# Key statistics counted a cycle earlier, the norms' bound in cycle 4, two banks for the last outputs, the verdict ahead of the last additions, and a looped general path

## The chip, the cores and the metric

The kernel runs on one core of one Trainium2 chip. The metric is the device time in microseconds (us) of that core: 1371.79 us is the median of three runs (1371.77, 1371.79 and 1372.5).

## What is computed

The input is `x` of 32 batches, each of 256 tokens with 256 channels, and a context of 32 batches of 77 tokens. Two gated blocks follow each other, all in float32:

```python
x = x + tanh(g_xattn) * attention(layernorm(x), ctx, ctx)   # 8 heads of 128
x = x + tanh(g_ffn)   * ffn(layernorm(x))                   # 16 heads of 16

# attention, for every head: no softmax over the keys
mixed = cw * cos(q, k) + vw * cos(q, k) * decorr + ww * ratio(q) * ratio(k)
ratio(f) = 2 * min(var(f), 1) / (var(f) + 1)      # of a head's 128 features
# cw, vw, ww, decorr: four numbers a head, from statistics over all batches

# ffn, for every head: a softmax over the queries
z = softmax(k q') v, heads side by side, times Wo
z = z / max(|z|, 1e-12)
z = z @ Wff
z = z / max(|z|, 1e-12)
x = x + tanh(g) * gelu(z)
```

Two things of it matter here. Of every key token and head the kernel needs the norm and the ratio, thus mean and variance of 128 features. And of the two normalizations at the end the first cancels in the second as long as neither norm meets its lower limit of 1e-12: the kernel multiplies Wo by Wff once and normalizes once. Whether that was allowed is judged at the end, from a bound on the norms. If it was not, a general path computes the end of the block again from what the kernel has kept in DRAM.

## The kernel before

**Order.** Five engines work side by side: PE multiplies into PSUM, ACT does the exponentials and some copies, DVE the rest of the elementwise work, POOL powers and scalings, SP issues the transfers. PE, ACT, DVE and POOL take their instructions in the order in which the program lists them (`InOrder`). SP's order is the framework's. So an instruction that waits holds up all that stand behind it on its engine.

**Stages.** A prologue computes the statistics over all batches. Then come software-pipelined cycles, one for each batch `n`. The list `cycle` names the stages of a cycle, each with the batch it works on relative to `n`: `(0, scores, 1)` is the feed-forward attention of batch `n`, `(1, ...)` the cross-attention of the next one, `(2, ...)` and `(3, ...)` the preparation of later ones, `(-1, ...)` the end of the last one. The two last batches have lists of their own, `last_but_one` and `last`. The function `run` calls a stage only once for each batch.

**The stages that the change touches or that stand around it.**

- `key_features(3)` computes features of keys by 128 rows, in the middle of a cycle, into `fvx` (four buffers). 77 rows to a batch and 128 to a tile: 20 tiles in all, the first two in the prologue, so 18 of the cycles have one to measure. `measure_keys(2)`, in the next cycle, runs `head_stats`: eight `bn_stats` (tile `kst`, one a head), then small operations on 128x8 values (tiles `kt`, `nrx`) on DVE and a power on POOL. `align_keys(2)` moves features and statistics to the batch's own rows by transfers of SP.
- Around `measure_keys` DVE has: the copy of `u` (`ff_out(-1)`), then the keys' operations, then `sums` and `vz` (`scale_values`), then the copy of `fq` out of PSUM (`query_features(2, 0, 1)`), whose bank PE writes again in `query_scores` (matmuls `mm<-fqT,fvT`).
- At the end of a cycle DVE has: two transposes `fb<-fq` (`turn_queries(2, 1)`), then `sums` and `vz` of `scale_values(0, 3)`, which waits for the last exponentials `e` of ACT. PE reads `vz` in `mix_values(-1, 3)` (matmuls `zp<-e,vz`), which opens the next cycle.
- `fetch_queries` brings the transposed query features back (`fqT<-fd`) for the `query_scores` of the next cycle.
- `ff_out` multiplies by the product of Wo and Wff (`mm<-w_of,zT`), both halves `t` of the tokens into one PSUM bank; ACT squares each half and sums it into `ny`, DVE copies the bank to `u`.
- `bound_norms` stands in `last`: ACT squares and sums two weights (tile `fb`), PE sums over the partitions (`mm<-bn,ones`), DVE makes the bound `low` of it. `judge`, after the last stage, compares all norms with it and leaves `verdict`, which every engine loads and branches on.
- `pass_time(n, k)` lets PE do `k` products that nobody reads (`mm<-winT,ident`). `last` has two of these.
- `mend`, the general path, is written out for all 32 batches behind the branch.
- `mm_tile` gives one of three PSUM banks in turn: a product waits until the third one before it was read.

Of the kernel before, what the change touches and what calls it, by code (L numbers as in the profile page):

```python
# [8 lines left out]
F32 = mybir.dt.float32  # L9
AF = mybir.ActivationFunctionType  # L10
# [4 lines left out]
P = 128  # L15
H = 8
# [19 lines left out]
def gated_block_kernel(  # L36
# [24 lines left out]
    nc = tc.nc  # L61
    B, S, D = x.shape
    M = cx.shape[1]
    NT = S // P
    NTOK = B * S
    NCTX = B * M
# [4 lines left out]
    pa = ctx.enter_context(tc.tile_pool(name="pa", bufs=2))  # L71
# [7 lines left out]
    pe, act, dve, pool = (  # L79
        InOrder(tc, e) for e in (nc.tensor, nc.scalar, nc.vector, nc.gpsimd)  # L80
    )
# [4 lines left out]
    o_v = out.rearrange("b (p t) d -> p b t d", t=NT)  # L86
# [31 lines left out]
    ny = const.tile([P, B, NT], F32, name="ny")  # L118
# [7 lines left out]
    def rsqrt_of(r, v):  # L126

        rows, n = v.shape
        pool.tensor_tensor(r, v, nhalf[0:rows, 0:n], ALU.pow)
# [11 lines left out]
    def mm_tile():  # L141
        return ps.tile([P, 512], F32, tag="mm", name="mm")

    def head_stats(src, rows, n, tag):

        st = pa.tile([rows, n, 6], F32, tag=f"{tag}st", name=f"{tag}st")
        for i in range(n):
            dve.bn_stats(st[:, i, :], src(i))
        t = pa.tile([rows, 4, n], F32, tag=f"{tag}t", name=f"{tag}t")
        s, d, m2, n2 = (t[:, i, :] for i in range(4))  # L150
        dve.tensor_tensor(s, st[:, :, 1], st[:, :, 4], ALU.add)
        dve.tensor_tensor(d, st[:, :, 1], st[:, :, 4], ALU.subtract)
        dve.tensor_tensor(m2, st[:, :, 2], st[:, :, 5], ALU.add)
        dve.scalar_tensor_tensor(d, d, P / 4.0, d, ALU.mult, ALU.mult)
        dve.scalar_tensor_tensor(s, s, P / 4.0, s, ALU.mult, ALU.mult)
        dve.tensor_tensor(m2, m2, d, ALU.add)
        dve.tensor_tensor(n2, m2, s, ALU.add)

        dve.tensor_scalar(d, m2, P - 1.0, None, ALU.add)
        dve.reciprocal(d, d)  # L160
        return m2, n2, d
# [26 lines left out]
    z_kept = dram.tile([P, B, 2, S], F32, tag="z_kept", name="z_kept", bufs=1)  # L188
    x_kept = dram.tile([P, B, NT, D], F32, tag="x_kept", name="x_kept", bufs=1)
# [4 lines left out]
    fvx = []  # L194
# [7 lines left out]
    def run(b, stage, *which):  # L202
        key = (b, stage.__name__, which)
        if key not in given:
            given.add(key)
            stage(b, *which)
# [62 lines left out]
    def halves_due(b):  # L269
        def least(b):  # L270
            return 2 * ((min(b, B - 1) * M + M - 1) // P + 1)

        return max(least(b), (least(b) + least(b + 1) + 1) // 2) if b >= 0 else 0
# [16 lines left out]
                )  # L290
            act.copy(fv[:, hh * 512 : (hh + 1) * 512], pf[0:rows, :])

    def measure_keys(b):

        for i in range(halves_due(b - 1) // 2, halves_due(b) // 2):
            rows = min(P, NCTX - i * P)
            fv = fvx[i % 4][0:rows]
            nr = nrx[0:rows, i % 4, :]
            m2, n2, rt = head_stats(lambda h: fv[:, h * P : (h + 1) * P], rows, H, "k")
            pool.tensor_tensor(nr[:, 0:H], n2, nquart[0:rows], ALU.pow)  # L300
            dve.scalar_tensor_tensor(nr[:, H : 2 * H], m2, P - 1.0, rt, ALU.min, ALU.mult)

# [136 lines left out]
    def scale_queries(b, t):  # L439

        k = kept[b]
        fq = k["fq", t]
        m2, n2, rt = head_stats(lambda h: fq[:, h * P : (h + 1) * P], P, H, "q")
        rq = pa.tile([P, H], F32, tag="rq", name="rq")
        rsqrt_of(rq, n2)
        fq_h = fq.rearrange("p (h d) -> p h d", d=P)
        pool.tensor_tensor(
            fq_h, fq_h, rq.unsqueeze(2).to_broadcast([P, H, P]), ALU.mult
        )
        dve.scalar_tensor_tensor(  # L450
            qrps[b % 2][t][:, :, MR], m2, P - 1.0, rt, ALU.min, ALU.mult
        )
# [209 lines left out]
    def ff_out(b):  # L662

        k = kept[b]
        pu = mm_tile()
        for t in range(NT):
            for c in range(2):
                pe.matmul(
                    pu[:, t * D : (t + 1) * D], lhsT=k["zT"][:, c, t * P : (t + 1) * P],
                    rhs=w_of[:, c, D : 2 * D], start=(c == 0), stop=(c == 1),  # L670
                )
        u = [P, NT, D], F32
        k["u"] = sw.tile(*u, tag="wf_n", name="u") if b == B - 1 else pa.tile(*u, tag="u", name="u")
        for t in range(NT):
            ge = pa.tile([P, D], F32, tag="ge", name="ge")
            act.activation(
                ge, pu[:, t * D : (t + 1) * D], AF.Square, accum_out=ny[:, b, t : t + 1]
            )
        dve.tensor_copy(k["u"].rearrange("p t c -> p (t c)"), pu)

    def ff_keep(b):

# [7 lines left out]
    def bound_norms(b):  # L690


        bn = pa.tile([P, 2], F32, tag="bn", name="bn")
        for i, w in enumerate((ffw["v"], w_of[:, :, 0:D])):
            ge = pa.tile([P, 2, D], F32, tag="fb", name="fb", bufs=2)
            act.activation(ge, w, AF.Square, accum_out=bn[:, i : i + 1])
        pt = mm_tile()
        pe.matmul(pt[:, 0:2], lhsT=ones, rhs=bn, start=True, stop=True)
        dve.tensor_copy(bn, pt[:, 0:2])
        dve.tensor_scalar(  # L700
            low, bn[:, 0:1], bn[:, 1:2], 4.0 * TINY * (S * D**0.5) ** 2, ALU.mult, ALU.mult
        )
        dve.tensor_scalar(low, low, LEAST, None, ALU.max)

    def judge():

        ok = pa.tile([P, B * NT], F32, tag="ge", name="ok")
        n_f = ny.rearrange("p b t -> p (b t)")
        dve.tensor_scalar(ok, n_f, low[:, 0:1], None, ALU.is_ge)
        dve.scalar_tensor_tensor(ok, n_f, MOST, ok, ALU.is_le, ALU.mult)  # L710
        dve.tensor_reduce(bad, ok, AX.X, ALU.min)
        pt = mm_tile()
        pe.matmul(pt[0:1, 0:1], lhsT=bad, rhs=ones[:, 0:1], start=True, stop=True)
        dve.tensor_scalar(verdict, pt[0:1, 0:1], -1.0, float(P), ALU.mult, ALU.add)

    def mend(b):
        zT = pa.tile([P, 2, S], F32, tag="zT", name="zT", bufs=1)
        nc.sync.dma_start(out=zT, in_=z_kept[:, b])
        xt = pa.tile([P, NT, D], F32, tag="x", name="x", bufs=8)
        nc.sync.dma_start(out=xt, in_=x_kept[:, b])  # L720
        for t in range(NT):
            pu = mm_tile()
            for c in range(2):
                pe.matmul(
                    pu, lhsT=zT[:, c, t * P : (t + 1) * P], rhs=w_of[:, c, :],
                    start=(c == 0), stop=(c == 1),
                )
            nn = pa.tile([P, 2], F32, tag="bn", name="nn")
            u = pa.tile([P, 2, D], F32, tag="u", name="u")
            act.activation(u[:, 0], pu[:, 0:D], AF.Square, accum_out=nn[:, 0:1])  # L730
            i1 = rsqrt(pa, nn[:, 0:1], 1, "rs2", least=TINY)
            dve.tensor_scalar(u[:, 0], pu[:, D : 2 * D], i1[:, 0:1], None, ALU.mult)
            act.activation(u[:, 1], u[:, 0], AF.Square, accum_out=nn[:, 1:2])
            i2 = rsqrt(pa, nn[:, 1:2], 1, "i2", least=TINY)
            act.activation(u[:, 0], u[:, 0], AF.Gelu, scale=i2)
            dve.scalar_tensor_tensor(xt[:, t], u[:, 0], tg[:, 1:2], xt[:, t], ALU.mult, ALU.add)
        nc.sync.dma_start(out=o_v[:, b], in_=xt)

    def ff_gelu(b):
        k = kept[b]  # L740
# [351 lines left out]
    for g in range(NG):  # L1092
# [4 lines left out]
        for i in range(4):  # L1097
            k = 4 * g + i
# [130 lines left out]
    def square_up(hh):  # L1229
# [17 lines left out]
        for i in range(4):  # L1247
# [3 lines left out]
            )  # L1251

    run(0, scale_queries, 0)
    square_up(0)
    run(0, query_features, 1, 0)
# [76 lines left out]
    for pair in (2, 0, 1):  # L1332
# [15 lines left out]
        (3, norm_inputs),  # L1348
        (0, exponents, 0, 0),
        (-1, ff_out),  # L1350
        (-1, ff_keep),
        (0, exponents, 0, 1),
        (2, measure_keys),
        (2, align_keys),
# [48 lines left out]
        (2, turn_queries, 1),  # L1403
        (2, fetch_queries, 0),
        (2, fetch_queries, 1),
        (0, scale_values, 3),
        (3, gain_inputs),
        (-1, ff_add),
# [8 lines left out]
        (0, exponents, 0, 1),  # L1417
        (0, scale_values, 0),
        (1, query_ratios),
        (-1, ff_norm_inv),  # L1420
        (0, scores, 1),
        (1, query_scores, 0),
# [37 lines left out]
        (0, scores, 1, 1),  # L1460
        (0, scale_values, 0),
        (0, exponents, 1, 0),
        (0, bound_norms),
        (0, scores, 2, 0),
        (0, exponents, 1, 1),
        (0, mix_values, 0),
# [16 lines left out]
        (-2, ff_gelu),  # L1483
        (-1, ff_gelu),
        (-2, ff_add),
        (0, ff_out),
        (0, ff_keep),
        (-1, ff_add),
        (0, ff_finish),
    ]  # L1490
    for n in range(-4, B):
        for ahead, stage, *which in {B - 2: last_but_one, B - 1: last}.get(n, cycle):
            if 0 <= n + ahead < B:
                run(n + ahead, stage, *which)
    judge()
    found = nc.values_load(verdict, min_val=0, max_val=P)
    with tc.If(found != 0):
        for b in range(B):
            mend(b)


# [32 lines left out]
```

## Time and profile before

One profiled execution of this program:

| | |
|---|---|
| time of the profiled execution | 1370.45 us |
| its span, first to last instruction | 1368.6 us |
| median of the three timed runs | 1371.79 us |
| mean granted PE clock | 0.987 |
| PE busy | 1315.4 us (96%) |
| DVE busy | 1042.4 us (76%) |
| ACT busy | 868.7 us (63%) |
| POOL busy | 509.7 us (37%) |
| chain that ended last, by engine | PE 80%, DVE 10%, ACT 5%, DMA 2%, POOL 1%, issue 1% |

The time is 1.85 us above the span. Busy shares are averages over stages with different limits, and a matmul's end is modelled, so 96% for PE does not say that PE has no waits. What a stage costs is read from its own rows: an idle time in brackets behind an instruction, with what ended it. All instructions of the four ordered engines show line 32, the helper that records them; they are told apart by their tiles, written `out<-in`. In the rows of sequencer instructions L1497 is the branch on the verdict and L1529 the end of the program.

### The profile page before, as it was taken

How to read it: one execution, taken by the hardware profiler on the slowest of the kernel's cores; microseconds unless marked ns; L12 is line 12 of the kernel's file. 1: busy time of each engine (PE TensorE's matmuls, PEld its weight loads, DVE VectorE, ACT ScalarE, POOL GpSimd, SP SyncE). 2: the span in 40 equal slices, each digit the busy share in tenths (PEclk: the TensorE clock that was granted, in tenths of full speed). 3: DMA queues.
4: the chain of work that ended last, by engine and by line, in shares of the span. 5: the costliest groups of instructions: out<-in, count | busy, mean ns of one | idle time of the engine just before them, and what ended most of it. 6: DMA issues, size and time to landing. Idle time of an engine off the chain costs nothing.

```text
span 1368.6 us, 26201 instructions
## 1 busy us (share of the span) xinstructions
PE 1315.4 (96%) x8775; PEld 802.1 (59%) x8775; DVE 1042.4 (76%) x3003; ACT 868.7 (63%) x2857; POOL 509.7 (37%) x633
## 2 busy tenths in 40 slices
PE   8999999999999999999999899999999998999994
PEld 7856555566655556556655565565656554665552
DVE  6747778787788787787787787877887876877853
ACT  6822566666666666676666567676667665766664
POOL 6824334333344333333343243433343333332300
PEclk9999999999999999999999999999999999999997
DMA  8610133333232333333332333333323233333200
GB/s 276 200 32 22 33 94 115 110 110 114 93 110 80 111 109 111 111 109 114 114 109 77 84 116 107 113 104 116 119 84 106 81 112 101 100 107 105 78 24 34
DMA packets 99645, 138.32 MB, mean 101 GB/s; under 512 B 14170, under 2 KB 65039, under 8 KB 99502
## 3 DMA queue, kind: packets, MB, share of 16 engines
q1 hardware_dynamic: 98670, 136.56, 32.0%
q8 instruction: 71, 1.16, 0.4%
q14 instruction: 72, 0.59, 0.1%
q10 hardware_dynamic: 832, 0.00, 0.0%
HBM read 62.04 MB, written 64.23 MB: 92 GB/s over the span
## 4 chain that ended last, share of the span: by engine, by line
PE 80%; DVE 10%; ACT 5%; DMA 2%; POOL 1%; issue 1%; ACTq 0%; POOLq 0%; SPq 0%
PE mm L32 61%; PE sc L32 10%; PE zp L32 9%; ACT e L32 3%; DVE nm L32 2%; DVE kst L32 2%; DVE kt L32 1%; ACT ge L32 1%; DVE u L32 1%; DVE fq L32 1%; DMA x<-in_x_dram 1%; DMA out_dram<-x 0%; DMA w_in_n<-in_L_xattn_w_in_dram 0%; DVE vz L32 0%; DMA ct<-in_ctx_dram 0%
## 5 line engine op out<-in xcount | busy, mean ns | idle before, releaser
L32 ACT ACTIVATE e<-sc,nm 128x256 f32<-128x256 f32 x1016 | 467.8, 483 | 219.7 <-DVE nm L32 219.7
L32 DVE TENSOR_REDUCE nm<-sc 128x4 f32<-128x1024 f32 x254 | 299.0, 1217 | 31.2 <-PE sc L32 31.2
L32 PE MATMUL mm<-winT,xTc 128*128 128x512 f32 x512 | 234.5, 599 | 0.0
L32 ACT ACTIVATION_READ_ACCUMULATOR e<-sc,nm 128x1 f32 x1016 | 219.3, 216 | 0.0
L32 POOL TENSOR_TENSOR rq<-qt,nhalf 128x8 f32<-128x8 f32 x64 | 105.2, 1644 | 250.9 <-DVE qt L32 250.9
L32 PE MATMUL sc<-q,kTf 32*128 32x512 f32 x1016 | 154.7, 645 | 3.4 <-ACT e L32 2.4
L32 PEld LDWEIGHTS mm<-winT,xTc 128*128 128x128 f32 x512 | 94.2, 190 | 104.7 <-issue 94.3
L32 PE MATMUL mm<-vw,s 128*128 128x256 f32 x640 | 147.0, 384 | 0.0
L32 PE MATMUL zp<-e,vz 128*32 128x256 f32 x2048 | 137.1, 386 | 1.8 <-DVE vz L32 1.8
L32 PEld LDWEIGHTS mm<-vw,s 128*128 128x128 f32 x640 | 118.9, 190 | 28.7 <-issue 13.5
L32 POOL TENSOR_TENSOR fq<-fq,rq 128x1024 f32<-128x1024 f32 x64 | 121.4, 1896 | 5.0
L32 PE MATMUL mm<-fqT,fvT 128*64 128x256 f32 (+2 forms) x1024 | 103.4, 401 | 20.4 <-DVE fq L32 12.2
L32 POOL TENSOR_TENSOR nrx<-kt,nquart 128x8 f32<-128x8 f32 (+1 forms) x20 | 33.2, 1661 | 225.3 <-DVE kt L32 225.3
L32 PEld LDWEIGHTS zp<-e,vz 128*32 128x32 f32 x2048 | 56.8, 110 | 90.0 <-issue 36.9
L32 DVE BATCH_NORM_STATS2 qst<-fq 128x6 f32<-128x128 f32 x512 | 104.6, 277 | 0.0
L32 PEld LDWEIGHTS mm<-fqT,fvT 128*64 128x64 f32 (+2 forms) x1024 | 47.4, 123 | 85.1 <-issue 27.4
L32 PE MATMUL mm<-woutT,fvT 128*64 128x256 f32 (+2 forms) x1024 | 93.7, 382 | 1.4 <-ACT v L32 1.4
L32 POOL TENSOR_SCALAR xn<-x,mv_x,rstd_x 128x256 f32<-128x256 f32 x64 | 78.6, 1236 | 4.2 <-issue 4.2
L32 ACT ACT_TABLE_LOAD x60 | 77.0, 1283 | 4.9 <-DMA x<-in_x_dram 4.3
L32 POOL TENSOR_SCALAR rs<-mv 128x1 f32<-128x1 f32 x64 | 14.4, 225 | 171.8 <-DVE mv L32 128.6
L32 ACT COPY s<-mm 128x512 f32<-128x512 f32 x64 | 31.0, 484 | 74.0 <-PE mm L32 74.0
L32 PE MATMUL mm<-winT,kT_all 128*128 128x512 f32 (+1 forms) x160 | 74.9, 598 | 0.0
(232 smaller groups left out, 2151.1 us busy)
## 6 DMA issues: line engine op xcount, KB each, us to landing
fd<-fb SPq DMA_DIRECT2D x60, 512.0 KB
fqT<-fd SPq DMA_DIRECT2D x240, 128.0 KB
x<-in_x_dram SPq DMA_DIRECT2D x64, 256.0 KB
x_kept<-x SPq DMA_DIRECT2D x32, 256.0 KB
z_kept<-zT SPq DMA_DIRECT2D x32, 256.0 KB
out_dram<-x SPq DMA_DIRECT2D x31, 256.0 KB
xd<-xb SPq DMA_DIRECT2D x29, 256.0 KB
xq<-xd SPq DMA_DIRECT2D x116, 64.0 KB
```

Of the source, the lines that this page charges most:

```text
L32: return lambda *args, **kw: self._tc.keep_in_program_order(method(*args, **kw))
```

## The change

It has six parts.

1. `head_stats` is split. `head_counts` issues the eight `bn_stats`, the rest stays in `head_stats`. A new stage `count_keys(3)` stands near the end of `cycle`, between `fetch_queries` and `scale_values(0, 3)`; `measure_keys(2)` in the next cycle finds the counts made. For the queries both parts still follow each other.
2. `bound_norms` is called in every cycle, after `ff_keep(-1)`, and works for `n = 4` alone. It leaves `last`.
3. `ff_out` of the last batch takes two PSUM banks, one for each half `t`, and copies `u` half by half.
4. `judge` stands ahead of `ff_finish` in `last`, and the addition of the batch before (`ff_add(-1)`) ahead of `ff_out`. The tile `ok` moves to the buffers of `fb`.
5. `last_but_one` gets `(0, pass_time, 4)` after `query_ratios`.
6. The general path becomes a loop over the 32 batches, with addresses from a register.

In the built program the order of SP's instructions up to the branch is the same as before, and so is POOL's. On DVE the eight `bn_stats` stand behind the transposes `fb` and ahead of `sums` at the end of a cycle. On PE `mm<-bn,ones` stands in cycle 4 between `mm<-w_of,zT` and `mm<-winT,xTc` (`query_features(2, 0, 0)`), on ACT the two squares `fb` stand between the squares of `ff_out` and the second half of the exponentials. The code behind the branch shrinks from 161 (PE, where each product becomes two weight loads and two matmuls in the profile), 225 (DVE), 258 (ACT), 320 (POOL) and 161 (SP) instructions of the built program's listing to between 26 and 46.

```diff
@@ -141,11 +141,15 @@
     def mm_tile():
         return ps.tile([P, 512], F32, tag="mm", name="mm")
 
-    def head_stats(src, rows, n, tag):
-
+    def head_counts(src, rows, n, tag):
         st = pa.tile([rows, n, 6], F32, tag=f"{tag}st", name=f"{tag}st")
         for i in range(n):
-            dve.bn_stats(st[:, i, :], src(i))
+            dve.bn_stats(st[:, i, :], src[:, i * P : (i + 1) * P])
+        return st
+
+    def head_stats(st, tag):
+
+        rows, n, _ = st.shape
         t = pa.tile([rows, 4, n], F32, tag=f"{tag}t", name=f"{tag}t")
         s, d, m2, n2 = (t[:, i, :] for i in range(4))
         dve.tensor_tensor(s, st[:, :, 1], st[:, :, 4], ALU.add)
@@ -290,13 +294,21 @@
                 )
             act.copy(fv[:, hh * 512 : (hh + 1) * 512], pf[0:rows, :])
 
-    def measure_keys(b):
+    key_stats = {}
+
+    def count_keys(b):
 
         for i in range(halves_due(b - 1) // 2, halves_due(b) // 2):
             rows = min(P, NCTX - i * P)
-            fv = fvx[i % 4][0:rows]
+            key_stats[i] = head_counts(fvx[i % 4][0:rows], rows, H, "k")
+
+    def measure_keys(b):
+
+        run(b, count_keys)
+        for i in range(halves_due(b - 1) // 2, halves_due(b) // 2):
+            rows = min(P, NCTX - i * P)
             nr = nrx[0:rows, i % 4, :]
-            m2, n2, rt = head_stats(lambda h: fv[:, h * P : (h + 1) * P], rows, H, "k")
+            m2, n2, rt = head_stats(key_stats.pop(i), "k")
             pool.tensor_tensor(nr[:, 0:H], n2, nquart[0:rows], ALU.pow)
             dve.scalar_tensor_tensor(nr[:, H : 2 * H], m2, P - 1.0, rt, ALU.min, ALU.mult)
 
@@ -440,7 +452,7 @@
 
         k = kept[b]
         fq = k["fq", t]
-        m2, n2, rt = head_stats(lambda h: fq[:, h * P : (h + 1) * P], P, H, "q")
+        m2, n2, rt = head_stats(head_counts(fq, P, H, "q"), "q")
         rq = pa.tile([P, H], F32, tag="rq", name="rq")
         rsqrt_of(rq, n2)
         fq_h = fq.rearrange("p (h d) -> p h d", d=P)
@@ -662,11 +674,14 @@
     def ff_out(b):
 
         k = kept[b]
-        pu = mm_tile()
+        pus = []
         for t in range(NT):
+            if t == 0 or b == B - 1:
+                pu = mm_tile()
+            pus.append(pu[:, t * D : (t + 1) * D])
             for c in range(2):
                 pe.matmul(
-                    pu[:, t * D : (t + 1) * D], lhsT=k["zT"][:, c, t * P : (t + 1) * P],
+                    pus[t], lhsT=k["zT"][:, c, t * P : (t + 1) * P],
                     rhs=w_of[:, c, D : 2 * D], start=(c == 0), stop=(c == 1),
                 )
         u = [P, NT, D], F32
@@ -674,9 +689,13 @@
         for t in range(NT):
             ge = pa.tile([P, D], F32, tag="ge", name="ge")
             act.activation(
-                ge, pu[:, t * D : (t + 1) * D], AF.Square, accum_out=ny[:, b, t : t + 1]
-            )
-        dve.tensor_copy(k["u"].rearrange("p t c -> p (t c)"), pu)
+                ge, pus[t], AF.Square, accum_out=ny[:, b, t : t + 1]
+            )
+        if b == B - 1:
+            for t in range(NT):
+                dve.tensor_copy(k["u"][:, t, :], pus[t])
+        else:
+            dve.tensor_copy(k["u"].rearrange("p t c -> p (t c)"), pu)
 
     def ff_keep(b):
 
@@ -690,6 +709,8 @@
     def bound_norms(b):
 
 
+        if b != 4:
+            return
         bn = pa.tile([P, 2], F32, tag="bn", name="bn")
         for i, w in enumerate((ffw["v"], w_of[:, :, 0:D])):
             ge = pa.tile([P, 2, D], F32, tag="fb", name="fb", bufs=2)
@@ -702,9 +723,9 @@
         )
         dve.tensor_scalar(low, low, LEAST, None, ALU.max)
 
-    def judge():
-
-        ok = pa.tile([P, B * NT], F32, tag="ge", name="ok")
+    def judge(b):
+
+        ok = pa.tile([P, B * NT], F32, tag="fb", name="ok", bufs=2)
         n_f = ny.rearrange("p b t -> p (b t)")
         dve.tensor_scalar(ok, n_f, low[:, 0:1], None, ALU.is_ge)
         dve.scalar_tensor_tensor(ok, n_f, MOST, ok, ALU.is_le, ALU.mult)
@@ -715,9 +736,9 @@
 
     def mend(b):
         zT = pa.tile([P, 2, S], F32, tag="zT", name="zT", bufs=1)
-        nc.sync.dma_start(out=zT, in_=z_kept[:, b])
+        nc.sync.dma_start(out=zT, in_=z_kept[:, bass.ds(b, 1)].squeeze(1))
         xt = pa.tile([P, NT, D], F32, tag="x", name="x", bufs=8)
-        nc.sync.dma_start(out=xt, in_=x_kept[:, b])
+        nc.sync.dma_start(out=xt, in_=x_kept[:, bass.ds(b, 1)].squeeze(1))
         for t in range(NT):
             pu = mm_tile()
             for c in range(2):
@@ -734,7 +755,7 @@
             i2 = rsqrt(pa, nn[:, 1:2], 1, "i2", least=TINY)
             act.activation(u[:, 0], u[:, 0], AF.Gelu, scale=i2)
             dve.scalar_tensor_tensor(xt[:, t], u[:, 0], tg[:, 1:2], xt[:, t], ALU.mult, ALU.add)
-        nc.sync.dma_start(out=o_v[:, b], in_=xt)
+        nc.sync.dma_start(out=o_v[:, bass.ds(b, 1)].squeeze(1), in_=xt)
 
     def ff_gelu(b):
         k = kept[b]
@@ -1349,6 +1370,7 @@
         (0, exponents, 0, 0),
         (-1, ff_out),
         (-1, ff_keep),
+        (0, bound_norms),
         (0, exponents, 0, 1),
         (2, measure_keys),
         (2, align_keys),
@@ -1403,6 +1425,7 @@
         (2, turn_queries, 1),
         (2, fetch_queries, 0),
         (2, fetch_queries, 1),
+        (3, count_keys),
         (0, scale_values, 3),
         (3, gain_inputs),
         (-1, ff_add),
@@ -1417,6 +1440,7 @@
         (0, exponents, 0, 1),
         (0, scale_values, 0),
         (1, query_ratios),
+        (0, pass_time, 4),
         (-1, ff_norm_inv),
         (0, scores, 1),
         (1, query_scores, 0),
@@ -1460,7 +1484,6 @@
         (0, scores, 1, 1),
         (0, scale_values, 0),
         (0, exponents, 1, 0),
-        (0, bound_norms),
         (0, scores, 2, 0),
         (0, exponents, 1, 1),
         (0, mix_values, 0),
@@ -1483,19 +1506,19 @@
         (-2, ff_gelu),
         (-1, ff_gelu),
         (-2, ff_add),
+        (-1, ff_add),
         (0, ff_out),
         (0, ff_keep),
-        (-1, ff_add),
+        (0, judge),
         (0, ff_finish),
     ]
     for n in range(-4, B):
         for ahead, stage, *which in {B - 2: last_but_one, B - 1: last}.get(n, cycle):
             if 0 <= n + ahead < B:
                 run(n + ahead, stage, *which)
-    judge()
     found = nc.values_load(verdict, min_val=0, max_val=P)
     with tc.If(found != 0):
-        for b in range(B):
+        with tc.For_i(0, B, 1) as b:
             mend(b)
```

## The prediction

> **What bounds the kernel now.** The chain of waits gives PE 80% of the span, DVE 10% and ACT 5%. So I look for idle time of PE, first in the list of waits.
>
> ```profile
> PE mm L32 <- DVE fq L32: 12.5, 17, 0.8
> PE mm L32 <- DMA out_dram<-x: 8.3, 2, 4.8
> ```
>
> PE idles 17 times, 0.8 us at the longest, for DVE's copy of `fq`, and twice for a transfer. The timeline of a cycle shows the first (start, duration, engine):
>
> ```profile
> 1066.43 0.69 DVE L32 COPY u<-mm 128x512 f32<-128x512 f32 x1 [1.65 <-ACT ge L32]
> ...
> 1067.04 1.64 DVE L32 BATCH_NORM_STATS2 kst<-fvx 128x6 f32<-128x128 f32 x8
> ...
> 1070.45 0.68 DVE L32 COPY fq<-mm 128x512 f32<-128x512 f32 x1
> ...
> 1071.18 2.07 PE L32 MATMUL mm<-fqT,fvT 128*64 128x256 f32 x24 [0.77 <-DVE fq L32]
> ```
>
> The counts and the small operations (1067.04 to 1070.01) hold back `sums`, `vz` and `fq`, and PE stands. The next view is the end of a cycle, where the counts go:
>
> ```profile
> 1093.74 2.36 DVE L32 STREAM_TRANSPOSE fb<-fq 128x1024 f32<-128x1024 f32 x2
> ...
> 1097.50 0.20 DVE L32 RECIPROCAL sums<-sums 128x8 f32<-128x8 f32 x1 [1.40 <-ACT e L32]
> 1097.73 0.29 DVE L32 TENSOR_TENSOR vz<-v,sums 128x128 f32<-128x128 f32 x1
> ...
> 1098.39 1.07 PE L32 MATMUL zp<-e,vz 128*32 128x256 f32 x16
> ```
>
> DVE is idle for 1.40 us there. Last, the end: the bound in `last`, the windows (start:end, length, PE busy, granted clock, DMA share, GB/s) around two idle times, and the branch on the verdict (duration, start).
>
> ```profile
> 1335.66 0.65 ACT L32 ACTIVATE fb<-w_v 128x512 f32<-128x512 f32 x1
> 1337.06 0.59 PE L32 MATMUL mm<-bn,ones 128*128 128x2 f32 x2 [2.91 <-ACT fb L32]
> ```
> ```profile
> 1298.20:1301.60 3.40, 1.99 (x10) 1.00 0.85 224
> 1301.60:1305.00 3.40, 2.42 (x6) 0.50 0.00 0
> 1332.30:1335.70 3.40, 1.85 (x8) 1.00 0.00 0
> 1335.70:1339.10 3.40, 2.04 (x6) 0.50 0.02 5
> ```
> ```profile
> L1497 PEldq COMPARE_BRANCH  x1: 3387/3387/3387, 1361.1 to 1361.1; - x1
> L1497 DVEq COMPARE_BRANCH  x1: 72/72/72, 1361.1 to 1361.1; - x1
> L1529 PEldq DRAIN  x2: 8/8/8, 1367.9 to 1368.2; - x2
> ```
>
> After a window in which PE had been busy for 1.99 or 1.85 of 3.40 us the clock stands at half for two windows. And PE, alone, needs 3.39 us for the branch and reaches its drain only at 1367.9, when SP, DVE, ACT and POOL have been through since 1365.1.
>
> **A. Counts a cycle earlier.** The copies of `u` start at 1029.27, 1066.43 and 1104.58. The first of these cycles has no counts and takes 37.16 us, the second has them and takes 38.15; PE has the same 256 matmuls in both. So a cycle pays 0.98 us. What stays, the operations on `kt` and `nrx`, takes 1.30 us (1068.71 to 1070.01). It then starts at 0.61 us after `u` and ends at 1.91, where `sums` without counts starts at 1.82 (1106.40 - 1104.58): 0.09 us late, covered by the 0.8 us that `fq` is early in a cycle without counts. At the new place the eight counts take 1.64 us against 1.40 idle, of which 0.16 is overlap at both ends (each group starts 0.08 before its forerunner ends): `vz` ends 0.08 us later, at 1098.10. PE takes it at 1098.39 and needs some 0.05 (1071.13 to 1071.18 for `fq`). Cover left: 0.24 us; if it is gone, each us on DVE is one on PE, 18 times. The key features were copied at 1087.9, nine us before, so no new wait; no transfer moves. 18 cycles have counts. Two of them stand for a transfer instead (3.45 and 4.82 us; the second begins with `fqT` fetched at 1144.1, seven us later than in other cycles) and resume when it lands, whatever DVE does: nothing to win. One is cycle 4, which is in B. 15 x 0.98 = **-14.7 us**; bounds 0 and -16.
>
> **B. The bound in cycle 4.** The product `mm<-bn,ones` waits for both squares of ACT, and on PE the query features of the next batches queue behind it. In the cycle with `u` at 299.46 ACT is through with the squares of `ff_out` at 299.29. By the rows above, PE gets the bound's product 1.40 us after the first square starts (1335.66 to 1337.06), at 300.69, and the next product 0.52 later (1337.58), at 301.21. Before, that product started at 297.18. PE loses 4.03 us. ACT's 1.22 us and DVE's three operations (0.55 us) lie inside this, as all that they hold up waits for PE too. The cold clock comes on top: the two cycles that stood 3.45 and 4.82 us took 43.20 and 43.68, thus 2.6 and 1.7 us beyond 37.16 and the wait. I take 2.1, bounds 0 and 3.4 (half of two windows). Less the 0.98 for counts: **+5.1 us**, bounds +3.1 and +6.4.
>
> **C. Products in `last_but_one`.** Four products of 128x256 are eight passes of 0.21 us, 1.7 us, after `mm<-ident,qrp` (ends 1299.06). The scores behind them start at 1300.8 in place of 1300.02, but the second half waits for ACT until 1302.58 anyhow: free. The window that held 1.99 us of work then holds some 3, and the clock should stay. With it the scores take 1.13 in place of 2.08 us, and 32 `mm<-fqT,fvT` 2.93 (1107.48 to 1110.41) in place of 4.75. These are on the chain, and `attend` then waits for ACT's last copy of `s`, which would be ready at about 1307.5 in place of 1309.8. **-2.5 us**; bounds 0 and -2.8. The Trainium skill, "TensorE: Matmul & The Clock Gate", section "Why this matters for your kernels", speaks against this part: only idle gaps above some 3 us cost the clock. By it these products would win nothing, as PE's gaps here are 0.96 and 1.42 us; the windows above show half clock all the same.
>
> **D. `last` without the bound.** Today: squares on ACT, 2.91 us of waiting on PE, half clock from 1335.7 to 1342.6. Without: the scores of step 2 follow at 1334.1 and end at 1335.2, and `nm` can follow `vz` at 1336.2. Then, by the same durations: maxima to 1337.4, exponentials to 1339.5; `mix_values(0)` from 1336.4, the next scores to 1338.9, their maxima 1338.5 to 1339.8, `vz` 1340.2, `mix_values(1)` to 1341.3, the last scores to 1342.4, four unread products to 1344.2, `mix_values(2)` to 1345.2, five more to 1347.6. The last exponentials end at 1345.6 and their `vz` at 1346.2, so PE is last, and `mix_values(3)` starts at 1347.6 in place of 1352.26. **-4.7 us**; bounds -2 (half clock again: two windows hold only some 60% work) and -6 (the last `vz`).
>
> **E. End and branch,** on today's clock. With its own bank the first half's square comes 0.9 us earlier, the second starts at 1355.50; the second power ends at 1357.2 (1358.18), its Gelu at 1357.7. DVE: second copy of `u` to 1356.5, three verdict operations 0.75, PE 0.35, verdict at 1357.7. The two additions wait behind it, with their stores: 1358.6 in place of 1359.23. SP issues the last store (0.33), then loads the verdict; from there to its last wait it took 2.4 us (1360.46 to 1362.85), so 1361.35, with 0.2 for the drain and 0.76 from the last drain to the end (1367.88 to 1368.64): 1362.3 in place of 1368.6. **-6.3 us**, if no engine has to fetch code. The jump goes over 26 to 46 instructions; today jumps over 225 (DVE) and 161 (SP) go through within 0.6 us, those over 258 (ACT) and more stand 3.4 to 4 us. If PE stands twice as now, it does so from 1358.3, and ends 3.6 us later: bounds -2.7 and -6.5. The Trainium skill, "Runtime: NRT & Kernel Launch", section "Instruction fetch mechanics", warns of loops: a taken branch stalls when its target lies outside the two code pages held. By that rule a loop that is not entered wins here, for its end lies near.
>
> **Sum.** -14.7 + 5.1 - 2.5 - 4.7 - 6.3 = -23.1 us: 1347.4 for the profiled execution (1370.45). The median, 1.34 above it, becomes 1348.7.
>
> **Rivals.** (1) *PE still fetches code at the branch.* For: today it does so twice, each 3.4 us, and the page borders of the new code are unknown. Against: the short jump. E falls to -2.7: 1352.3. (2) *The clock falls in the last cycles all the same*; the windows' phase is not known. For: five idle times today brought half clock. Against: the rebuilt rows hold more work. D falls to -2 and C to -1: 1352.9. (3) *The counts bring nothing*, as the 1.30 us that stay are enough to keep `fq` late, or `vz` takes as much back. Against: 0.09 and 0.24 us above. A is 0: 1363.4. (4) *Slower: the counts run at half pace at the new place*, where POOL normalizes (1094.36 to 1096.82) during their first part. The 1.64 us more, less the cover of 0.24, reach PE 18 times: (1.64 - 0.24) x 18 = 25.2 us, a net +2.1: 1373.9. It decides from counts of 3.2 us on; at 4 us the kernel stands at 1388. Against: the same instruction takes 1.63 us in all 64 groups of the queries.
>
> **How the numbers follow.** Chances: forecast 0.64, (1) 0.11, (2) 0.13, (3) 0.08, (4) 0.04. The forecast's own bounds are 1345 (B without cold clock, C at its bound) to 1351 (B at its bound, D at -4); (1) and (2) together would give 1356.5. So 1345 to 1357 leaves out (3), (4) and a little at the low end. 0.2% or 2.7 us is about what a measurement of this kernel can tell from no change. All cases but (4) are faster by more: 0.95; (4) is split, 0.02 within the bound and 0.03 slower.
>
> **What would show it.** A: PE's wait for `fq` gone from the list, cycles of 37.2 us, `sums` behind the counts with no idle time. B: one cycle of 43 us, with PE idle some 3.5 us for ACT's `fb`. C and D: no window at half clock between 1290 and the end of the products, `mix_values(3)` 4.7 us nearer to the start of `last`. E: PE's branch under 0.1 us and a drain within 1.5 us of it. The forecast is wrong if `sums` starts more than 0.3 us later after `fb` than now, or if PE's branch takes 3.4 us again.

## The result, and the profile after

The changed kernel takes 1350.9 us in the median of four runs (1350.2 to 1354.2) against 1371.8 for the kernel before: a ratio of 0.9851, 95% interval 0.9834 to 0.9868. Run again later it gave 0.9851 (0.9826 to 0.9876). So it is some 1.5% faster. The forecast was 1348.7, range 1345 to 1357. The profiled execution (1350.83) spans 1348.9 us, 19.7 less than before.

PE's list of waits (total, times, longest) has lost its first line, the 17 waits for `fq`. Cycle 4's wait for the bound has come in, and the two for a transfer are still there (lines 2 to 5 of the list; the transfer named as what ended a wait is inferred, and the trial "Rows that divide" below shows which ones it was).

```profile
PE mm L32 <- DMA z_kept<-zT: 5.4, 1, 5.4
PE mm L32 <- DMA out_dram<-x: 3.6, 1, 3.6
PE zp L32 <- DVE vz L32: 3.4, 2, 2.1
PE mm L32 <- ACT fb L32: 3.4, 1, 3.4
```

The timeline at the end of a cycle shows the counts at their new place, between the transposes and `sums`:

```profile
1048.88 2.36 DVE L32 STREAM_TRANSPOSE fb<-fq 128x1024 f32<-128x1024 f32 x2
...
1051.17 1.60 DVE L32 BATCH_NORM_STATS2 kst<-fvx 128x6 f32<-128x128 f32 x8
...
1052.69 0.18 DVE L32 RECIPROCAL sums<-sums 128x8 f32<-128x8 f32 x1
1052.90 0.29 DVE L32 TENSOR_TENSOR vz<-v,sums 128x128 f32<-128x128 f32 x1
...
1053.53 1.07 PE L32 MATMUL zp<-e,vz 128*32 128x256 f32 x16
```

DVE no longer idles there, and the eight counts take 1.60 us, as long as at their old place. `vz` ends at 1053.19, and the 16 `zp` start 0.34 us later, when PE is through with the products before them; the counts hold nothing up. Next, cycle 4: the first square and PE's product, with what it waited for.

```profile
298.67 0.66 ACT L32 ACTIVATE fb<-w_v 128x512 f32<-128x512 f32 x1
...
300.07 0.38 PE L32 MATMUL mm<-bn,ones 128*128 128x2 f32 x2 [3.36 <-ACT fb L32]
```

The granted clock is 1.00 or 0.50, and in all traces here half clock between the prologue and the last products comes in whole windows of 3.41 us. Windows (start:end, length, PE busy, PEld, DVE, ACT, POOL, granted clock, DMA share, GB/s), the first two after the unread products of `last_but_one`, the other two in `last`:

```profile
1291.57:1294.99 3.42, 2.68 (x13) 0.76 (x11) 1.76 (x4) 2.28 (x11) 0.95 (x2) 1.00 0.20 74
1294.99:1298.40 3.41, 3.41 (x18) 1.68 (x16) 1.69 (x2) 1.42 (x6) 0.00 (x0) 0.50 0.00 0
1329.12:1332.53 3.41, 2.19 (x22) 0.72 (x20) 2.85 (x6) 3.41 (x16) 0.00 (x0) 1.00 0.00 0
1332.53:1335.95 3.42, 3.42 (x28) 2.30 (x27) 1.62 (x3) 3.02 (x15) 0.00 (x0) 1.00 0.00 0
```

Half clock followed the busier of the two windows. Last, the end: PE's branch (ns), SP's last waits and drain, and the packets between 1345.75 and 1347.6.

```profile
L1520 PEldq COMPARE_BRANCH  x1: 367/367/367, 1343.8 to 1343.8; - x1
...
L1552 SPq EVENT_SEMAPHORE  x10: 17/28/28, 1345.8 to 1348.9; - x10
...
L1552 SPq DRAIN  x3: 7/7/7, 1348.1 to 1348.4; - x3
```
```profile
q8 instruction: 1, 0.02, 3.2%
q1 hardware_dynamic: 9, 0.01, 2.7%
```

PE goes through its branch in 0.37 us. But SP, which stands at its last waits from 1345.8, reaches its drain only at 1348.1. In between the last store's other packets have ended (by 1345.7), a code block of 16,384 bytes moves for 0.95 us from 1345.82, and then eight rows of the store, 1 KB each, and its 4-byte semaphore write come one after another from 1346.75 to 1347.46. SP's list of waits has the store as what ended its last wait:

```profile
SPq L1552 <- DMA out_dram<-x: 1.8, 1, 1.8
```

Where the 19.7 us came from, stretch by stretch (us, differences of the two profiled executions; cycles run from one copy of `u` to the next):

| Part | Forecast | Measured |
|---|---|---|
| up to the first copy of `u` | 0 | +1.3 (186.02 to 187.33) |
| A: 15 cycles with counts | -14.7 | -14.5 (38.15 to 37.17 in most) |
| cycles 16 and 26, which wait for a transfer | 0 | +0.1 (-0.78, +0.87) |
| B: cycle 4 | +5.1 | +4.4 (38.15 to 42.57) |
| C: the stretch behind the query scores of `last_but_one` | -2.5 | -1.1 (33.27 to 32.19) |
| D: from there to `mix_values(3)` of `last` | -4.7 | -4.7 (18.26 to 13.59) |
| E: from there to the end | -6.3 | -5.3 (16.38 to 11.10) |

### The profile page after: what moved, and what is told of

Its sections match the earlier page's. It is cut to its first block, busy times and chain, and to the rows that moved or that the text cites. A ratio compares the mean times of both kernels' runs of the same rounds, so it can differ in the third digit from the quotient of the medians.

```text
span 1348.9 us, 26215 instructions
## 1 busy us (share of the span) xinstructions
PE 1309.8 (97%) x8783; PEld 802.7 (60%) x8783; DVE 1039.8 (77%) x3004; ACT 870.1 (64%) x2857; POOL 510.4 (38%) x633
## 4 chain that ended last, share of the span: by engine, by line
PE 90%; DVE 4%; DMA 2%; ACT 2%; POOL 1%; issue 1%; SPq 0%; ACTq 0%; DVEq 0%; POOLq 0%
PE mm L32 70%; PE sc L32 11%; PE zp L32 9%; DVE nm L32 1%; ACT e L32 1%; DMA x<-in_x_dram 1%; DMA w_in_n<-in_L_xattn_w_in_dram 1%; DVE st L32 1%; DMA ct<-in_ctx_dram 0%; DVE qt L32 0%; DVE qst L32 0%; ACT ge L32 0%; POOL rstd_x L32 0%; DMA gcol<-in_L_xattn_ln_g_dram 0%; DMA out_dram<-x 0%
## 5 line engine op out<-in xcount | busy, mean ns | idle before, releaser
L32 PE MATMUL sc<-q,kTf 32*128 32x512 f32 x1016 | 151.3, 640 | 1.7 <-ACT kTf L32 1.0
L32 PE MATMUL mm<-fqT,fvT 128*64 128x256 f32 (+2 forms) x1024 | 99.1, 397 | 8.9 <-DMA z_kept<-zT 5.4
L32 POOL TENSOR_SCALAR rs<-mv 128x1 f32<-128x1 f32 x64 | 14.5, 226 | 181.5 <-DVE mv L32 138.5
L32 ACT COPY fvx<-mm 128x512 f32<-128x512 f32 (+1 forms) x40 | 23.4, 586 | 80.2 <-PE mm L32 80.2
```

What stands on the lines that cost most here:

```text
L32: return lambda *args, **kw: self._tc.keep_in_program_order(method(*args, **kw))
```

## Experiments

Each kernel is the changed one with the edit shown. Times are medians beside the kernel before on the same chip; ratios are to that kernel.

**Counts back (A).**

```diff
-        (3, count_keys),
```

> The changed kernel, but the counts of the keys are back behind the copy of u, where they were before (they are no longer a step of their own). Theory: the counts' place alone makes 37.17 us out of 38.15 in every cycle that has counts. Then PE's waits for fq of 0.76 us are back in 15 to 17 cycles, those cycles take 38.15 us, and the kernel takes 1350.9 + 15 x 0.98 = 1365.6 us. Rival: the shorter cycles come from another part of the change (order of the steps, the split of the statistics itself); then the cycles stay at 37.17 us and the time within 2 us of 1350.9.

Measured: 1362.9 us, ratio 0.9931 (0.9907 to 0.9956). PE's first wait is back:

```profile
PE mm L32 <- DVE fq L32: 11.7, 16, 0.8
```

Cycles with counts take 38.15 or 38.16 us again, the others 37.17. The rival falls: the place of the counts is the whole of A. Cycle 4 took 42.57 us with its counts at the old place too, so there PE's wait for the bound hides them. The time rose by 12 us and not by 14.7 since in the profile other stretches were shorter: the one up to the first copy of `u` by 1.2 us, and the one behind the query scores, 30.51 us, by 1.7 (see below).

**Bound back in `last` (B and D).**

```diff
 cycle:
-        (0, bound_norms),
 last:
         (0, exponents, 1, 0),
+        (0, bound_norms),
```

> The changed kernel, but the norms' bound is back in the last phase, at its place of before; all else stays. Theory: cycle 4 gives back all that the bound costs there, 42.57 - 37.17 = 5.4 us, and the last phase pays what it saved, the 4.7 us by which its fourth mixing of values came nearer to its start (18.3 us after the copy of u before, 13.6 after). Sum -0.7 us: 1350.2, no difference that can be measured; moving the bound was worth nothing. Rival: the last phase is shorter because of the clock or of the products of last_but_one, not because the bound left; then its fourth mixing stays at 13.6 us after the copy of u and the time is 1345.5 us.

Measured: 1351.3 us, ratio 0.9829 (0.9807 to 0.985), no difference from the changed kernel. Cycle 4 took 37.16 us (5.4 less) and `last` came to `mix_values(3)` 21.28 us after the copy of `u` (7.7 more), of which half clock in four windows is a part:

```profile
1317.24:1320.65 3.41, 0.68 (x4) 0.60 (x6) 2.12 (x6) 3.41 (x16) 0.72 (x1) 1.00 0.00 0
1320.65:1324.06 3.41, 3.41 (x24) 0.83 (x24) 1.52 (x3) 1.75 (x9) 0.00 (x0) 0.50 0.00 0
1324.06:1327.48 3.42, 1.86 (x8) 0.28 (x8) 1.51 (x4) 2.02 (x9) 0.00 (x0) 0.50 0.00 0
```

So the bound did what D says, and the rival falls. But the change, as B and D had forecast, only moved the wait of 2.9 us to a place where it is 3.4 us: 5.4 paid in cycle 4, counted without its keys' counts, for 4.7 to 7.7 saved.

**Bound in two steps.** Squares where ACT idles, the product later.

```diff
-        (0, bound_norms),                 # behind ff_keep
...
         (2, query_features, 1, 1),
+        (0, bound_norms),                 # squares on ACT only
         (0, scores, 2),
         (0, exponents, 2, 0),
         (0, mix_values, 1),
+        (0, bound_product),               # PE's product, three DVE operations
```

> The changed kernel with the bound of cycle 4 in two steps: the two squares on ACT stand ahead of the third scores, where ACT idles for 3.5 us (426.7 to 430.2 in cycle 7 of the changed kernel's trace), and the product and the three operations on DVE stand behind the second mixing of values, two us or more after the squares' end. Theory: the 5.4 us that cycle 4 pays are PE's wait for the squares and the half clock after it, not the work; nothing waits now and the cycle takes 37.2 to 37.5 us: 1350.9 - 5.4 = 1345.5. Rival: ACT's 1.3 us and DVE's 0.5 us hold back what stands behind them wherever they are; then PE loses 1 to 3 us at another place of the cycle and the time is 1347 to 1349.

Measured: 1344.9 us, ratio 0.9798 (0.9776 to 0.982). Cycle 4 takes 37.38 us:

```profile
306.57 0.63 ACT L32 ACTIVATE fb<-w_v 128x512 f32<-128x512 f32 x1
...
309.72 0.38 PE L32 MATMUL mm<-bn,ones 128*128 128x2 f32 x2
```

The same work with no wait behind it costs 0.2 us in place of 5.4.

**Rows that divide.**

```diff
-            nc.sync.dma_start(out=k["fv"][at : at + n], in_=fvx[i % 4][row : row + n])
+            one = 1 if n in (71, 73) else 0
+            nc.sync.dma_start(out=k["fv"][at : at + n - one], in_=fvx[i % 4][row : row + n - one])
+            if one:
+                nc.sync.dma_start(out=k["fv"][at + n - 1 : at + n], in_=fvx[i % 4][row + n - 1 : row + n])
```

> The changed kernel, but a copy of 71 or 73 rows of key features is issued as one of 70 or 72 rows and one of a single row. Theory: the two long cycles (42.42 and 44.55 us) exist because a copy with a prime number of rows moves on one DMA engine, at 24.6 KB/us, with the turned queries queued behind it on that engine; 72 = 8 x 9 and 70 = 7 x 10 rows divide, both waits (3.55 and 5.37 us) and the half clock after them go, the cycles take 37.2 and 37.4 us: 1350.9 - 5.25 - 7.14 = 1338.5. Rival: the rate is that of the source's partitions or of two copies in one queue, not of the row count; then the waits stay and the time is 1350 to 1352 (two more issues on SP).

Measured: 1339.05 us, ratio 0.9747 (0.9719 to 0.9774). Cycles 16 and 26 take 37.16 us each. GB/s in 40 slices of 0.4 us, from half a us after the copy of 73 rows is issued, first the changed kernel, then this one (72 rows and 1):

```profile
GB/s 236 164 143 21 20 20 10 0 31 10 31 20 31 20 31 20 31 31 20 338 338 399 369 410 358 277 143 61 31 31 20 31 20 31 20 31 31 20 31 20
```
```profile
GB/s 236 164 164 184 257 219 76 12 0 0 0 0 0 0 0 0 0 0 0 379 399 389 410 399 420 225 46 230 279 292 230 228 197 223 218 205 207 233 228 343
```

In the first row the copy trickles before and after the burst of the turned queries (338 and on), one packet of 4 KB behind the other, 0.16 us each and some 25 GB/s; the fetch of the queries, which needs all turned queries landed, is issued only at 754.7. In the second row the copy is through before the burst, and the fetch (230 and on) follows at once. The Trainium skill states the rule ("DMA: Bandwidth & Descriptors", section "Why a DMA increments its semaphore by 16 and not by 1"): a copy is spread over the largest number of engines, up to 16, that divides the outer size of both its sides, so one with a prime size above 16 lies on one engine. These rows agree, though the trace does not number the engines; that the queries' share waits behind the copy on that engine is inferred from this.

**Both.**

> The changed kernel with the bound in two steps and the copies of 71 and 73 rows divided. Theory: the three waits lie in different cycles and add up: 1350.9 - 5.4 - 12.4 = 1333.1, below both kernels, with every cycle at 37.2 to 37.4 us or, where two halves of keys are made, 38.9, and no half clock between 200 and 1280 us. Rival: with the waits gone another transfer or engine is late; then a cycle stays over 40 us and the time over 1338.

Measured: 1333.2 us, ratio 0.9717 (0.9695 to 0.974); run again later, with the expectation

> The same kernel without these products, beside it on the same chip. Theory: half clock at the waits of the end is drawn in most runs; spread as before, 1328.7 to 1335, median 1333. Rival: the spread was that of the first chip; then all runs lie within 1 us of each other.

1333.5 us, ratio 0.9713 (0.97 to 0.9727), runs from 1328.9 to 1334.8. The waits add up. PE's list in the first profile, whose only wait over 1.9 us (2.2) is in `last`:

```profile
PE sc L32 <- ACT xna L32: 4.8, 5, 1.8
PE zp L32 <- DVE vz L32: 3.4, 2, 2.2
PE mm L32 <- DVE bad L32: 1.8, 1, 1.8
```

**No products (C), and the clock.**

```diff
 last_but_one:
-        (0, pass_time, 4),
```

> The changed kernel without the four unread products in last_but_one. Theory: they keep one of two windows at full clock; without them the clock is at half for two windows after that place, and the stretch from there to the copy of u that begins the last phase is 1.1 us longer (33.3 in place of 32.2 us): 1352 us. Rival: the clock does what it did whether the products are there or not, and where the window's borders fall decides; then the stretch takes 32.2 us or less and the time is 1350.9 or up to 1 us below.

Measured: 1350.35 us, ratio 0.9828 (0.9805 to 0.985); the stretch took 32.19 us, as with the products, with half clock in one window (1295.0 to 1298.4). The forecast of two windows and 33.3 us failed, and the rival held: in this run the products do nothing. The other profiles say more, since the windows lie differently in each. Measured from the border of a window to the start of PE's last `mm<-ident,qrp`, the ten profiles with four products divide: at 1.50, 1.56, 1.61 and 1.94 us half clock follows and the stretch takes 32.1 to 32.2 us; at 0.42, 0.68, 0.71, 1.35, 2.14 and 2.38 it does not, and the stretch takes 30.5. The kernel before, without products, stood at 0.60 and had half clock in two windows (33.27); no_products stood at 1.88, where it follows with products too. So with the products the position in the window goes with whether half clock follows, and a run draws its position. That the products hold the clock at some positions rests on 0.60 against 0.68 and 0.71 alone, one profile of a kernel that differs in other ways too; what they are worth is not shown, and the ratios with and without them (0.9851 and 0.9828) have overlapping intervals.

The unaltered kernel was run beside these:

> The changed kernel once more, unaltered, beside the others on their chip. Theory: its waits are fixed by the program, the half clock after each depends on how the windows of 3.41 us lie, which changes from run to run; so its runs spread over 4 us (1350.2 to 1354.2 the first time), and in the profile the cycles without a wait repeat to 0.02 us, while cycles 4, 16 and 26 and the stretch after the last query scores differ by up to 2 us from the first profile. Rival: the spread comes from the transfers of the prologue; then the cycles repeat and the copy of u that begins the first cycle moves.

1350.4 us, runs from 1348.9 to 1355.1. Both hold in part: most cycles without a wait repeat (37.16 us), of the places named only cycle 16 differs (43.92 in place of 42.42), and the first copy of `u` came at 185.38 us in place of 187.33. In the other profiles it came at 184.9 to 186.3, in the kernel before at 186.02. The 1.3 us of the prologue that the forecast lacked thus belong to the execution, not to the change.

```diff
-        (0, pass_time, 4),
+        (0, pass_time, 6),
```

> The changed kernel with six unread products in place of four at the place in last_but_one. Theory: with four, PE still waits 0.74 us for the second half of the scores, and it depends on the window whether half clock follows (it did in three of six profiles with four products); with six PE waits at most 0.1 us, no half clock follows, and the stretch up to the copy of u of the last phase takes 30.5 to 30.7 us. Rival: the wait does not decide over the clock, or the longer products hold the scores back; then half clock follows in this profile (32.1 us), or the stretch takes 31 us or more at full clock.

(Half clock had followed in three of eight such profiles by then, not of six.) Measured: 1354.7 us, ratio 0.9868 (0.9852 to 0.9884); the profiled run was the lowest (1350.2). In it PE has no wait at the place and the stretch takes 30.50 us, but it stood at 2.47 us in its window, close to 2.38, where four products had sufficed as well; and `last` had half clock in two windows (16.81 us to `mix_values(3)` in place of 13.59). Why the other three runs lie at 1354.5 and above is open, as they have no profile; the trial does not decide.

```diff
 last_but_one:
+        (0, pass_time, 6),  # for 4
 last, ahead of mix_values 0 and 1:
+        (0, pass_time, 4),
+        (0, pass_time, 2),
```

> The kernel with the bound in two steps and the copies divided, with unread products in the three waits of PE that are left at the end: six in place of four ahead of the query scores in last_but_one, four more ahead of the first mixing of values in last (wait 2.15 us) and two ahead of the second (1.22 us). Theory: what is left of the spread (1328.7 to 1334.9) is half clock that some runs draw at these waits; with PE busy there no run draws it, the profile has no half clock between 200 us and the last products, and the runs lie at 1328.5 to 1330. Rival: the products themselves are in the way of the scores or the half clock has another cause; then the median stays at 1332 or above.

Measured, on the kernel with both edits: 1331.4 us, ratio 0.9691 (0.9678 to 0.9705), runs from 1328.8 to 1332.0. The spread is half that of the kernel beside it (3.1 against 5.9 us), but half clock was still drawn in one window of `last`. The edit did more than was meant: a step with the same arguments runs once per batch, so the four products that had stood ahead of the third mixing fell away, PE waited there,

```profile
1314.05 1.07 PE L32 MATMUL zp<-e,vz 128*32 128x256 f32 x16 [1.76 <-DVE vz L32]
```

and the window from 1315.23 on is at half clock. So this trial moved a wait and does not show what filling all three would bring; the median lies between what the forecast (1328.5 to 1330) and the rival (1332 or above) had said. It is the lowest of all medians here, but its interval overlaps that of the kernel with both edits (0.97 to 0.9727). Both are some 1.5% under the changed one (0.9691 and 0.9713 against 0.9851).

**The end (E).**

```diff
-        with tc.For_i(0, B, 1) as b:
+        for b in range(B):
             mend(b)
```

> The changed kernel with the general path written out 32 times again in place of the loop. Theory: the far jump is what makes PE fetch code twice, 3.4 us each, after the verdict: PE's branch from 1343.8 on takes 3.4 us, its drain comes at about 1350.6 in place of 1344.4, and the end 0.8 us after that: +2.5 us, 1353.4. Rival: PE's two waits depended on where the code lay in the blocks that are fetched, not on the length of the jump; then PE's branch stays at 0.4 us and the time at 1350.9, as SP's wait for the last store ends last.

Measured: 1352.2 us, ratio 0.9855 (0.9827 to 0.9883).

```profile
L1520 PEldq COMPARE_BRANCH  x1: 4528/4528/4528, 1341.9 to 1341.9; - x1
```

PE stands 4.53 us at the far jump, and 0.36 to 0.37 us in each of the twelve profiles with the loop: this wait comes with the length of the jump, as forecast. But PE stood once and not twice as in the kernel before, although the body is written out as there; its drain came at 1346.6. What made the second wait there is open, so the rival, the place of the code, is not excluded for it. And the time from `mix_values(3)` to the end was 11.76 us, only 0.66 more than with the loop, because with the loop the end waits for the last store, which lands 9.6 us after `mix_values(3)` starts in both. The expected 2.5 was wrong.

```diff
-        (0, judge),
         (0, ff_finish),
+        (0, judge),
```

> The changed kernel with the verdict behind the last additions again. Theory: the last wait is now for the landing of the last store, 3.9 us after SP takes it up, and the verdict ahead of the additions holds that store back: without it the second addition ends at 1343.65 in place of 1344.02 (the copy of u that opens the first cycle at 187.33), the store is taken up at 1343.7 and the time from the start of the fourth mixing of values to the end is 10.7 us in place of 11.1. Rival: the verdict, now 1.5 us later on every engine, becomes the last; then that stretch is 11.5 us or more.

Measured in a single run: 1348.2 us; from `mix_values(3)` to the end 9.67 us in place of 11.10.

```profile
L1552 SPq EVENT_SEMAPHORE  x10: 17/28/28, 1344.8 to 1346.1; - x10
...
L1552 SPq DRAIN  x3: 7/7/7, 1345.3 to 1345.6; - x3
```
```profile
q8 instruction: 1, 0.02, 5.6%
q14 instruction: 1, 0.01, 2.0%
```

The direction was right and the size was not (0.4 expected, 1.4 measured). SP's last waits now take 0.5 us: all rows of the last store are through by 1343.7, and the 16 KB code block comes behind them (between 1343.7 and 1345.4 only code moves). The store's second issue came 0.4 us earlier, as expected, but its last packet landed 2.4 us earlier. In the changed kernel the block came ahead of eight rows of the store. So it did in all twelve profiles with the verdict ahead of the additions: the block moves for 0.95 to 1.84 us, and the eight rows begin within 0.02 us of its end. In the eleven of them with the loop this stretch takes 10.4 to 11.2 us, so the 9.67 stands apart although it is one run. The verdict ahead of the additions, one part of the change, thus costs some 1.4 us.

## Why the prediction came out as it did

**A** was right in mechanism and size: 0.98 us a cycle, nothing given back at the new place, where the cover of 0.24 us was enough.

**B** was right in mechanism. PE's product came 1.23 us after the copy of `u`, where the forecast had it; the next product followed 0.25 us later and not 0.52, and the half clock, taken as 2.1 us, cost 1.7. These are the two mis-sized terms. Of the eight profiles with the bound at this place two had no half clock in cycle 4, which then took 40.87 us: work and wait cost 3.7 us, where 4.03 was forecast. Five had one window (42.5 to 42.6 us) and one had two (43.87), thus 1.7 and 3.0 us of half clock, inside the bounds 0 and 3.4 that B gave it.

**C** failed in the profiled run at "the clock should stay": the window's work rose, to 2.68 of 3.41 us (some 3 forecast), yet half clock followed in one of the two windows, and -2.5 became -1.1. Even this 1.1 is not shown to be the products': without them the stretch took the same 32.19 us. In the six profiles with four products where half clock did not follow, the stretch is 2.8 us shorter than before. The step took busy time in a window as what decides; a window with 2.68 us of work lost the clock and one with 2.19 kept it. Rival (2) was thus half true, in one of its two places. The Trainium skill ("TensorE: Matmul & The Clock Gate", section "Why this matters for your kernels") names gaps above some 3 us, one idle window, as what costs the clock, and the prediction read this as only such gaps. PE's one wait there was 0.74 us, and half clock followed it in four of ten profiles, so longer gaps are not the only ones that cost the clock here. The forecast's rule did not hold either, and what decides within a window stays open.

**D** was right to 0.1 us in this run, and its steps with it: `mix_values(0)` to `(2)` start 2.31, 6.25 and 10.23 us after the copy of `u`, where 2.4, 6.2 and 10.2 follow from the forecast. That no half clock came is partly luck: of the twelve profiles without the bound in `last`, those of bound_split, even_rows, six_products and both_warm had some and reached `mix_values(3)` 2 to 5.6 us later.

**E** had two right steps: the short jump frees PE (4.5 us without the loop, 0.37 with it, under 0.1 forecast), and the verdict is there 5.4 us after `mix_values(3)` starts. The step that failed is "from there to its last wait it took 2.4 us", plus 0.2 for the drain: SP loaded the verdict 6.7 us after `mix_values(3)` starts, as forecast, but took 3.6 us from there to its drain (1344.51 to 1348.14). The 2.4 came from a kernel in which the last store had landed (by 1360.6) some 2 us before SP stood at its last wait (1362.8). Here SP's last wait is for the store itself, with a code block ahead of its last rows, and the end came 1.0 us later than forecast. The step "The two additions wait behind it" was noted and priced only by its delay of the store's issue, not by what the store would meet.

**The prologue** was not in the sum; its 1.3 us are the execution's. With C and E (1.4 and 1.0 us) it makes up most of the 3.4 us by which the profiled execution missed its 1347.4, less the 0.7 of B. The median missed by 2.2 only, and that is luck: the 1.34 us between profiled execution and median were carried over from the kernel before, and here they are 0.07. The rivals (1), (3) and (4) did not occur. Two sums of the prediction are off and change nothing: counts of 4 us would give 1387 and not 1388, and the low bound of 1345 needs A at its bound too, as B and C alone give 1346.4.

## What to carry to other kernels

Moving work that an engine waits for does not remove the wait; look for the place where the engine that does it idles, and let the consumer come later (5.4 us became 0.2). The row counts of copies deserve a look at the trace: two transfers with a prime number of rows cost 12 us here, more than anything else that was left. At a kernel's end, look at what the last store meets: here it was 1.4 us better to issue it ahead of the work for the branch, so that it landed before the code block came.

## What was not expected of the hardware

A code block of 16 KB, fetched around the branch at the end, moved ahead of the last eight rows of a store and held back its completion by some 1.8 us (1345.68 to 1347.46). A wait of PE of 0.74 us can be followed by 3.4 us at half clock, depending on where it falls in a window; a wait of 2.15 us in `last` went without it in eight of the eleven profiles that have it.
